# Layer 3's sums of neighbours as seven products of halves instead of eight

## Chip, cores and metric

The kernel runs on one core of one Trainium2 chip. The metric is the device time of one execution in microseconds, taken as the median of several runs. A profile of one execution goes with it.

## The reference

Four graph layers run one after the other over `x` (16 batches of 1024 nodes and 256 features) and `adj` (16 matrices of 1024 x 1024), all in float32. Each layer works on the normalised, rectified `x` and adds its result to `x`. The change lies in the last layer only:

```python
h = jnp.maximum(_layernorm(x, axis=-1), 0.0)
neighbor_sum = jnp.einsum('bnm,bmd->bnd', adjacency, h)
agg = epsilon * h + neighbor_sum
h = jnp.einsum('bnd,dh->bnh', agg, W1) + b1          # 256 -> 1024
h = jax.nn.silu(_rmsnorm(h, rms_weight))
out = jnp.einsum('bnh,hd->bnd', h, W2) + b2          # 1024 -> 256
x = x + out
```

## The kernel before

Layers 0 and 1 run first over all batches, then layer 2, which is a recurrence over the nodes, then layer 3 (`layer_3`, from L1093), which takes the last quarter of the time. Layer 3 is a loop over the 16 batches. For batch b it has these stages:

- **load** (L1130): the queue of SyncE fetches `x`, the layer-2 result `hn`, and the transposed adjacency in two halves of 512 columns, each a tile of 128 partitions x 8 row tiles x 512 (2 MB, four DMAs). The halves rotate over three buffers: two named `bxt`, one named `at`. A half is loaded when the products that read its buffer's last content are done.
- **prepare** (L1149): adds `hn` to `x` (VectorE, L1163), takes mean and variance (L1166, L1167), the inverse root on GpSimd (`rs`, L83), `shift` on VectorE (L1171), eight relus on ScalarE into `h` (L1173), and on GpSimd epsilon on the diagonal of the adjacency (L1154) and the output bias into `x` (L1177).
- **sums** (L1180): `agg` transposed, that is 256 features x 1024 nodes, as four parts (two halves of features by two halves of nodes). A part is eight products, one for each row tile, summed in a PSUM bank (L1189), copied to `ag` by ScalarE (L1191). VectorE forms the four differences `tt` that the next stage wants (L1195 to L1199).
- **inner** (L1202): the product with W1. It is written as seven products of halves in place of eight, in a loop of four steps with seven products each (L1210). `ws` and a changed quarter of W1 hold the combinations of the weights, made once (L1118 to L1121). Every result is evicted by VectorE into `hh` (L1214), with partial sums `u2` and `u3` (L1229, L1231) and ScalarE's copy `p1` (L1226). ScalarE squares each result (L1216, tile `sq`, two buffers) and GpSimd adds the squares up (L1218, 14 additions a batch). PSUM has five banks under the name `ph`, which sums and inner share.
- **norm** (L1241): four transposes for each of the two `ss` (L1250), a reduction (L1251), the inverse root on GpSimd, transposes of it (L1258), 16 scalings by VectorE (L1261) and 16 SiLUs by ScalarE (L1262).
- **outer** (L1265): the product with W2, again as seven products of halves with 16 small products each (L1279). VectorE makes the combinations of `hh` (L1273, eight operations of 128 x 1024, one of them into the buffer `s1`), and the results are added to `x` by VectorE and GpSimd (L1297 to L1312). The DMA of the output is issued from GpSimd's queue (L1337).

The loop of L1321 runs inner of batch b, then sums of batch b+1 with norm of batch b between its parts, then outer of batch b, which calls prepare of batch b+2 in its middle. The program is written in this order; the framework's scheduler then moves instructions on their engines by its own estimates of their durations, so the order of VectorE and GpSimd in the built program is not quite that of the text. [...]

Of the kernel before, what the change touches and what calls it, by code (L numbers as in the profile page):

```python
# [9 lines left out]
F32 = mybir.dt.float32  # L10
AF = mybir.ActivationFunctionType
ALU = mybir.AluOpType
# [4 lines left out]
P = 128  # L17
B, N, D, H = 16, 1024, 256, 1024
NT = N // P
DC = D // P  # L20
# [20 lines left out]
def gnn_stack(ctx: ExitStack, tc: tile.TileContext, a: dict, out: bass.AP):  # L41
    nc = tc.nc
# [29 lines left out]
    def rows(ap):  # L72
        return ap.rearrange("(t p) d -> p t d", p=P)
# [1019 lines left out]
    def layer_3(shared, x, hn, at, h, eye):  # L1093
        with ExitStack() as st:
            wp = st.enter_context(tc.tile_pool(name="w3", bufs=1))
            big = st.enter_context(tc.tile_pool(name="big3", bufs=2))
            small = st.enter_context(tc.tile_pool(name="small3", bufs=2))
            psum = st.enter_context(tc.tile_pool(name="psum3", bufs=2, space=PSUM))
# [14 lines left out]
            NH = 512  # L1113
# [3 lines left out]
            a11, a12, a21, a22 = (w1[:, c, p * HH * P : (p + 1) * HH * P] for p in range(2) for c in range(2))  # L1117
            nc.gpsimd.tensor_tensor(ws[:, 0], a21, a22, ALU.add)  # L1118
            nc.gpsimd.tensor_tensor(ws[:, 1], ws[:, 0], a11, ALU.subtract)
            nc.gpsimd.tensor_tensor(a21, a11, a21, ALU.subtract)  # L1120
            nc.gpsimd.tensor_tensor(ws[:, 2], a12, ws[:, 1], ALU.subtract)  # L1121

            wt = wp.tile([P, 3, HH, P], F32, name="wt")
# [6 lines left out]
            def load(b):  # L1130
                if b:
                    x[b] = big.tile([P, NT, D], F32, name="x", bufs=3)
                    nc.sync.dma_start(x[b], rows(x2_d[b]))
                    hn[b] = shared.tile([P, NT, D], F32, name="hb")
                    nc.sync.dma_start(hn[b][:, : NT - 1], rows(hn_d[b])[:, : NT - 1])
                    nc.sync.dma_start(hn[b][:, NT - 1], hs_d[NT - 1][b // GB][b % GB * P : (b % GB + 1) * P])
                    at[b] = []
                while len(at[b]) < N // NH:
                    n0 = NH * len(at[b])

                    if (2 * b + len(at[b])) % 3 < 2:
                        half = shared.tile([P, NT, NH], F32, name="bxt")
                    else:
                        half = big.tile([P, NT, NH], F32, name="at", bufs=1)
                    for t in range(0, NT, 2):
                        nc.sync.dma_start(half[:, t : t + 2], rows(a["adjT"][b])[:, t : t + 2, n0 : n0 + NH])
                    at[b].append(half)
# [29 lines left out]
                    nc.gpsimd.tensor_tensor(to[:, t : t + 2], x[b][:, t : t + 2], b2[:, None].to_broadcast([P, 2, D]), ALU.add)  # L1177
                x[b] = to

            def sums(b):  # L1180

                ag = big.tile([P, DC, N], F32, name="ag", bufs=1)
                tt = big.tile([P, 4, NH], F32, name="tt", bufs=1)
                b21 = []

                def part(n0, c):
                    pa = psum.tile([P, NH], F32, name="ph", bufs=5)
                    for mt in range(NT):
                        nc.tensor.matmul(pa, h[b][:, mt, c * P : (c + 1) * P], at[b][n0 // NH][:, mt],  # L1189
                                         start=mt == 0, stop=mt == NT - 1)  # L1190
                    nc.scalar.copy(ag[:, c, n0 : n0 + NH], pa)  # L1191
                    if (n0, c) == (0, 1):
                        b21.append(pa)
                    if (n0, c) == (NH, 0):
                        nc.vector.tensor_sub(tt[:, 0], pa, ag[:, 0, :NH])  # L1195
                    if (n0, c) == (NH, 1):
                        nc.vector.tensor_sub(tt[:, 1], pa, tt[:, 0])
                        nc.vector.tensor_sub(tt[:, 2], pa, ag[:, 0, NH:])
                        nc.vector.tensor_sub(tt[:, 3], b21[0], tt[:, 1])  # L1199
                return (ag, tt), [lambda n0=n0, c=c: part(n0, c) for n0 in range(0, N, NH) for c in range(DC)]  # L1200

            def inner(ag, tt):  # L1202

                hh = [big.tile([P, HC, NH], F32, name=f"hh{q}", bufs=1) for q in range(2)]
                ss = [small.tile([P, NH], F32, name=f"ss{q}", bufs=1) for q in range(2)]
                begun = [False, False]

                def product(lhsT, rhs, onto=None):
                    ph = onto if onto is not None else psum.tile([P, NH], F32, name="ph", bufs=5)
                    nc.tensor.matmul(ph, lhsT, rhs, start=onto is None, stop=True, skip_group_check=onto is not None)  # L1210
                    return ph

                def result(k, q, ph, u):
                    nc.vector.scalar_tensor_tensor(hh[q][:, k], ph, b1[:, k : k + 1], u, op0=ALU.add, op1=ALU.add)  # L1214
                    sq = small.tile([P, NH], F32, name="sq") if begun[q] else ss[q]
                    nc.scalar.activation(sq, hh[q][:, k], AF.Square)  # L1216
                    if begun[q]:
                        nc.gpsimd.tensor_tensor(ss[q], ss[q], sq, ALU.add)  # L1218
                    begun[q] = True

                left = lambda: None
                for k in range(HH):
                    mine = slice(k * P, (k + 1) * P)
                    p1, u2, u3 = (small.tile([P, NH], F32, name=name) for name in ("p1", "u2", "u3"))
                    ph = product(a11[:, mine], ag[:, 0, :NH])
                    nc.scalar.copy(p1, ph)  # L1226
                    left()
                    ph = product(ws[:, 1, mine], tt[:, 1])
                    nc.vector.tensor_add(u2, ph, p1)  # L1229
                    ph = product(a21[:, mine], tt[:, 2])  # L1230
                    nc.vector.tensor_add(u3, ph, u2)  # L1231
                    p5 = product(ws[:, 0, mine], tt[:, 0])
                    result(HH + k, 1, p5, u3)
                    result(HH + k, 0, product(a22[:, mine], tt[:, 3]), u3)
                    result(k, 0, product(a12[:, mine], ag[:, 1, :NH]), p1)
                    left = lambda k=k, mine=mine, p5=p5, u2=u2: result(
                        k, 1, product(ws[:, 2, mine], ag[:, 1, NH:], p5), u2)
                left()
                return hh, ss

            def norm(hh, ss):  # L1241

                got = {}

                def mean():
                    all_ = small.tile([P, N // P], F32, name="all")
                    for q in range(2):
                        pq = psum.tile([P, NH // P, P], F32, name="po", bufs=3)
                        for n in range(NH // P):
                            nc.tensor.transpose(pq[:, n], ss[q][:, n * P : (n + 1) * P], ident)  # L1250
                        nc.vector.tensor_reduce(all_[:, q * NH // P : (q + 1) * NH // P], pq, AX.X, ALU.add)  # L1251
                    got["rms"] = inv_sqrt(small, all_, RMS_EPS, [P, N // P], "rms", mul=1.0 / H)

                def spread():
                    for q in range(2):
                        pr = psum.tile([P, NH], F32, name="po", bufs=3)
                        for n in range(4):
                            nc.tensor.transpose(pr[:, n * P : (n + 1) * P],  # L1258
                                                got["rms"][:, 4 * q + n : 4 * q + n + 1].to_broadcast([P, P]), ident)
                        for k in range(HC):  # L1260
                            nc.vector.tensor_mul(hh[q][:, k], hh[q][:, k], pr)  # L1261
                            nc.scalar.activation(hh[q][:, k], hh[q][:, k], AF.Silu, scale=rw[:, k : k + 1])  # L1262
                return mean, spread
# [50 lines left out]
            load(0)  # L1314
            prepare(0)
            load(1)
            ags, parts = sums(0)
            for part in parts:
                part()
            prepare(1)  # L1320
            for b in range(B):  # L1321
                if b + 2 < B:
                    load(b + 2)
                hh, ss = inner(*ags)
                mean, spread = norm(hh, ss)
                parts = [lambda: None] * 4
                if b + 1 < B:
                    ags, parts = sums(b + 1)
                parts[0]()
                mean()  # L1330
                parts[1]()
                spread()
                parts[2]()
                parts[3]()

                outer(b, hh, (lambda: prepare(b + 2)) if b + 2 < B else (lambda: None))
                nc.gpsimd.dma_start(rows(out[b]), x[b])  # L1337

    layers_0_1()
    with tc.tile_pool(name="shared", bufs=2) as shared:  # L1340
        x, hn, at, h = {}, {}, {}, {}
# [49 lines left out]
```

## Time and profile before

| | |
|---|---|
| median of 3 runs | 4627.27 us (4623.85 to 4629.18) |
| span of the profiled execution, first to last instruction | 4622.5 us |
| median less that span | 4.8 us |
| TensorE busy, of the span | 4336.9 us (94%) |
| VectorE busy | 2535.5 us (55%) |
| GpSimd busy | 1623.5 us (35%) |
| ScalarE busy | 1279.5 us (28%) |
| first product of layer 3's sums | 3334.9 us |
| one batch of layer 3 in the steady state | 78.3 us |
| in it: TensorE, VectorE, GpSimd, ScalarE busy | 78.3, 51.6, 34.4, 28.9 us |
| granted clock of TensorE, mean | 0.978 |

The profiled execution's own time is its span with the launch and the end around it, which the records do not show; against the median of the runs these make up 4.8 us. A row of a timeline gives the start in us from the span's start, the duration in us, engine, line, operation, output and inputs with their shapes, how many in a row (x), and in brackets the idle time before it with what ended it. PE is TensorE, DVE VectorE, ACT ScalarE, POOL GpSimd. A float32 product stands in the records as two matmuls.

### The profile page before, as it was taken

How to read it: one execution, taken by the hardware profiler on the slowest of the kernel's cores; microseconds unless marked ns; L12 is line 12 of the kernel's file. 1: busy time of each engine (PE TensorE's matmuls, PEld its weight loads, DVE VectorE, ACT ScalarE, POOL GpSimd, SP SyncE). 2: the span in 40 equal slices, each digit the busy share in tenths (PEclk: the TensorE clock that was granted, in tenths of full speed). 3: DMA queues.
4: the chain of work that ended last, by engine and by line, in shares of the span. 5: the costliest groups of instructions: out<-in, count | busy, mean ns of one | idle time of the engine just before them, and what ended most of it. 6: DMA issues, size and time to landing. Idle time of an engine off the chain costs nothing. (4 is left out here: it accounts for less than half of the span.)

```text
span 4622.5 us, 54868 instructions
## 1 busy us (share of the span) xinstructions
PE 4336.9 (94%) x19223; PEld 2956.2 (64%) x19223; DVE 2535.5 (55%) x6436; ACT 1279.5 (28%) x2741; POOL 1623.5 (35%) x1914
## 2 busy tenths in 40 slices
PE   8999799999997899999999999999799999999998
PEld 4444345555554687778787878787655656565656
DVE  6667944555554344444444444445356666676765
ACT  1111111221121232323232323233234333333333
POOL 3222333433333333332332323234244444445352
PEclk9999899999998999999999999999899999999999
DMA  4333244455544644454444454542142222232310
GB/s 150 112 116 100 73 112 146 164 194 188 156 145 154 196 138 154 131 166 141 154 121 151 131 159 135 167 144 73 55 142 89 100 92 92 88 104 82 110 46 19
DMA packets 530989, 576.78 MB, mean 125 GB/s; under 512 B 42544, under 2 KB 439472, under 8 KB 528304
## 3 DMA queue, kind: packets, MB, share of 16 engines
q1 hardware_dynamic: 499536, 460.27, 32.0%
q0 software_dynamic: 31040, 111.44, 6.9%
q8 instruction: 206, 3.38, 0.3%
q14 instruction: 207, 1.70, 0.1%
HBM read 469.65 MB, written 116.65 MB: 127 GB/s over the span
## 5 line engine op out<-in xcount | busy, mean ns | idle before, releaser
L295 PE MATMUL pa<-at,h 128*128 128x512 f32 x1088 | 495.3, 608 | 33.0 <-DVE ag L300 33.0
L295 PE MATMUL pa<-at,q 128*128 128x512 f32 x960 | 423.6, 594 | 0.0
L623 PE MATMUL pf<-hb,ab 128*128 128x256 f32 x1568 | 407.9, 383 | 14.5 <-DMA hb<-hs_d 5.7
L295 PEld LDWEIGHTS pa<-at,h 128*128 128x128 f32 x1088 | 209.7, 196 | 277.6 <-issue 231.5
L735 PE MATMUL pf<-hs,wx 128*128 128x256 f32 x1536 | 348.9, 381 | 19.2 <-POOL hs L726 17.6
L735 PEld LDWEIGHTS pf<-hs,wx 128*128 128x128 f32 x1536 | 290.6, 191 | 62.5 <-POOL hs L726 19.4
L623 PEld LDWEIGHTS pf<-hb,ab 128*128 128x128 f32 x1568 | 280.3, 191 | 67.2 <-issue 14.2
L295 PEld LDWEIGHTS pa<-at,q 128*128 128x128 f32 x960 | 178.2, 190 | 215.9 <-issue 212.8
L1189 PE MATMUL ph<-bxt,hb 128*128 128x512 f32 x704 | 310.8, 597 | 3.8 <-ACT hb L1173 3.0
L1218 POOL TENSOR_TENSOR ss<-ss,sq 128x512 f32<-128x512 f32 x224 | 280.7, 1271 | 87.1 <-ACT sq L1216 83.4
L1023 POOL DMA_INDIRECT hs_d<-h,table x128 | 129.6, 1013 | 330.0 <-ACTq L1009 150.8
L1279 PEld LDWEIGHTS po<-w,hh 128*128 128x128 f32 x2048 | 235.9, 193 | 9.5 <-issue 7.2
L1279 PE MATMUL po<-w,hh 128*128 128x128 f32 x2048 | 240.1, 277 | 1.4 <-ACT hh L1262 0.7
L1189 PEld LDWEIGHTS ph<-bxt,hb 128*128 128x128 f32 x704 | 133.2, 192 | 164.7 <-issue 159.8
L740 DVE TENSOR_TENSOR gates<-pf,bias 128x512 f32<-128x512 f32 x128 | 88.3, 691 | 238.6 <-PE pf L735 238.6
L1261 DVE TENSOR_TENSOR hh<-hh,po 128x512 f32<-128x512 f32 x256 | 154.5, 681 | 96.7 <-PE po L1258 96.7
L83 POOL TENSOR_TENSOR rs<-rs_v,mhalf 128x8 f32<-128x8 f32 (+1 forms) x65 | 106.9, 1645 | 255.0 <-DVE rs_v L79 241.5
L771 PE MATMUL pf<-bd,h 128*128 128x384 f32 (+4 forms) x512 | 185.6, 454 | 5.3 <-ACT bs L610 2.8
L1216 ACT ACTIVATE sq<-hh 128x512 f32<-128x512 f32 x224 | 141.1, 630 | 164.3 <-DVE hh L1214 125.6
L830 ACT ACTIVATE r<-pr 128x256 f32<-128x256 f32 (+3 forms) x230 | 68.1, 348 | 403.5 <-PE pr L789 389.5
L1214 DVE SCALAR_TENSOR_TENSOR hh<-ph,b,u 128x512 f32<-128x512 f32 x192 | 144.0, 751 | 64.9 <-PE ph L1210 54.8
L774 DVE TENSOR_TENSOR bxt<-bxt,pf 128x384 f32<-128x384 f32 (+4 forms) x256 | 125.0, 501 | 97.0 <-PE pf L771 95.5
(296 smaller groups left out, 8473.1 us busy)
## 6 DMA issues: line engine op xcount, KB each, us to landing
at<-in_adjT SPq DMA_DIRECT2D x64, 1024.0 KB, 7.1
ab<-in_adj SPq DMA_DIRECT2D x128, 512.0 KB, 4.3
bxt<-in_adjT SPq DMA_DIRECT2D x88, 512.0 KB, 6.7
at<-in_adjT SPq DMA_DIRECT2D x40, 512.0 KB, 6.8
ad<-in_adj SPq DMA_DIRECT2D x128, 128.0 KB, 6.2
x_d<-x POOLq DMA_DIRECT2D x16, 1024.0 KB, 5.1
he_d<-h POOLq DMA_DIRECT2D x16, 1024.0 KB, 8.9
heT_d<-hT POOLq DMA_DIRECT2D x16, 1024.0 KB, 4.2
```

The source lines that it names most:

```text
L295: nc.tensor.matmul(pa, h[:, mt, c * P : (c + 1) * P], at[n0 // 512][:, mt], start=mt == 0, stop=mt == NT - 1)
L623: nc.tensor.matmul(pb, ab[:, jts[k]], hb[:, jts[k]], start=k == 0, stop=k == len(jts) - 1)
L735: nc.tensor.matmul(pg[:, e], wx[:, c, q * D + e * P : q * D + (e + 1) * P], self.hs[:, c], start=c == 0, stop=c == DC - 1)
L771: nc.tensor.matmul(pf, h[:, g, c * P : (c + 1) * P], bd[:, g, b0 : b0 + n, S : S + far], start=True, stop=True)
L774: return lambda: nc.vector.tensor_add(to, to, pf)
L1023: nc.gpsimd.indirect_dma_start(out=hs_d[t][g][:, :], out_offset=row(1, g, t, s), in_=h[:, g], in_offset=None)
L1189: nc.tensor.matmul(pa, h[b][:, mt, c * P : (c + 1) * P], at[b][n0 // NH][:, mt], start=mt == 0, stop=mt == NT - 1)
L1214: nc.vector.scalar_tensor_tensor(hh[q][:, k], ph, b1[:, k : k + 1], u, op0=ALU.add, op1=ALU.add)
L1216: nc.scalar.activation(sq, hh[q][:, k], AF.Square)
L1218: nc.gpsimd.tensor_tensor(ss[q], ss[q], sq, ALU.add)
L1261: nc.vector.tensor_mul(hh[q][:, k], hh[q][:, k], pr)
L1279: nc.tensor.matmul(po[:, n], left[:, c, n * P : (n + 1) * P], right[:, c], start=onto is None and n == 0 and c == 0, stop=c == HH - 1, ski ...
```

## The change

The sums of neighbours are written as seven products of quarters instead of eight. The 1024 source nodes and the 1024 target nodes of the adjacency are halved: b11, b21 are the upper and lower half of the rows of the left tile, b12, b22 those of the right tile. m0 and m1 are the two halves of the rows of `h`, each with two halves of columns. A product is now four matmuls of 128x128 by 128x512, and there are seven for a batch: 28 in place of 32.

- **Combinations of h** (`combined`): four subtractions or additions of 128 x 512 on GpSimd, three into the new tile `hs` and one in place.
- **Combinations of the adjacency**: b12 becomes b11 + b12 by a DMA from GpSimd's queue that adds to its destination within SBUF (L1199). t2 = that + b22, then t1 = t2 - b11 (in b12's place), then t2 = t2 + b21, all on VectorE in two operations of 128 x 1024 each (L1187). t2 lives in the buffer `s1` that outer uses too.
- **Results**: ScalarE makes three copies of 128 x 512 (before: four), VectorE seven evictions or subtractions (before: four). What is subtracted changes so that `tt` comes out negated in part, for which one combination of W1 changes its sign.
- **Order**: `combined` of batch b+1 is called ahead of inner of batch b; its two remaining steps, the DMA and t2, are handed to inner and called in the second and third step of its loop. In the built program the scheduler puts the DMA further ahead: on GpSimd behind `rms` of the batch before. It puts t2's two halves into VectorE's list behind `rs_v` and behind the second `u` of outer, and GpSimd's addition L1307 (now L1360) ahead of `rs`.

```diff
@@ -1117,7 +1117,7 @@
             a11, a12, a21, a22 = (w1[:, c, p * HH * P : (p + 1) * HH * P] for p in range(2) for c in range(2))
             nc.gpsimd.tensor_tensor(ws[:, 0], a21, a22, ALU.add)
             nc.gpsimd.tensor_tensor(ws[:, 1], ws[:, 0], a11, ALU.subtract)
-            nc.gpsimd.tensor_tensor(a21, a11, a21, ALU.subtract)
+            nc.gpsimd.tensor_tensor(a21, a21, a11, ALU.subtract)
             nc.gpsimd.tensor_tensor(ws[:, 2], a12, ws[:, 1], ALU.subtract)
 
             wt = wp.tile([P, 3, HH, P], F32, name="wt")
@@ -1177,29 +1177,80 @@
                     nc.gpsimd.tensor_tensor(to[:, t : t + 2], x[b][:, t : t + 2], b2[:, None].to_broadcast([P, 2, D]), ALU.add)
                 x[b] = to
 
-            def sums(b):
+            def quarters(b):
+                left, right = at[b]
+                return left[:, : NT // 2], right[:, : NT // 2], left[:, NT // 2 :], right[:, NT // 2 :]
+
+            def add(engine, to, left, right, op):
+                for k in range(0, NT // 2, 2):
+                    two = slice(k, k + 2)
+                    engine.tensor_tensor(to[:, two], left[:, two], right[:, two], op)
+
+            def combined(b):
+                b11, b12, _, b22 = quarters(b)
+                m0, m1 = h[b][:, : NT // 2], h[b][:, NT // 2 :]
+                hs = big.tile([P, 3, NT // 2, P], F32, name="hs", bufs=1)
+                nc.gpsimd.tensor_tensor(hs[:, 0], m0[:, :, P:], m1[:, :, P:], ALU.subtract)
+                nc.gpsimd.tensor_tensor(hs[:, 1], hs[:, 0], m0[:, :, :P], ALU.subtract)
+                nc.gpsimd.tensor_tensor(m0[:, :, P:], m0[:, :, :P], m0[:, :, P:], ALU.subtract)
+                nc.gpsimd.tensor_tensor(hs[:, 2], m1[:, :, :P], hs[:, 1], ALU.add)
+                t2 = big.tile([P, NT // 2, NH], F32, name="s1", bufs=1)
+                return (t2, hs), [lambda: nc.gpsimd.dma_start(b12, b11, accum_op=ALU.add),
+                                  lambda: add(nc.vector, t2, b12, b22, ALU.add)]
+
+            def sums(b, t2, hs):
 
                 ag = big.tile([P, DC, N], F32, name="ag", bufs=1)
                 tt = big.tile([P, 4, NH], F32, name="tt", bufs=1)
-                b21 = []
-
-                def part(n0, c):
-                    pa = psum.tile([P, NH], F32, name="ph", bufs=5)
-                    for mt in range(NT):
-                        nc.tensor.matmul(pa, h[b][:, mt, c * P : (c + 1) * P], at[b][n0 // NH][:, mt],
-                                         start=mt == 0, stop=mt == NT - 1)
-                    nc.scalar.copy(ag[:, c, n0 : n0 + NH], pa)
-                    if (n0, c) == (0, 1):
-                        b21.append(pa)
-                    if (n0, c) == (NH, 0):
-                        nc.vector.tensor_sub(tt[:, 0], pa, ag[:, 0, :NH])
-                    if (n0, c) == (NH, 1):
-                        nc.vector.tensor_sub(tt[:, 1], pa, tt[:, 0])
-                        nc.vector.tensor_sub(tt[:, 2], pa, ag[:, 0, NH:])
-                        nc.vector.tensor_sub(tt[:, 3], b21[0], tt[:, 1])
-                return (ag, tt), [lambda n0=n0, c=c: part(n0, c) for n0 in range(0, N, NH) for c in range(DC)]
-
-            def inner(ag, tt):
+                b11, t1, b21, b22 = quarters(b)
+                m0, m1 = h[b][:, : NT // 2], h[b][:, NT // 2 :]
+                got = {}
+
+                def product(left, right, onto=None):
+                    pa = onto if onto is not None else psum.tile([P, NH], F32, name="ph", bufs=5)
+                    for k in range(NT // 2):
+                        nc.tensor.matmul(pa, left[:, k], right[:, k], start=onto is None and k == 0, stop=k == NT // 2 - 1,
+                                         skip_group_check=True)
+                    return pa
+
+                def room(name):
+                    return small.tile([P, NH], F32, name=name)
+
+                def first():
+                    got["pa"] = product(m0[:, :, :P], b11)
+                    got["p1"] = room("p1")
+                    nc.scalar.copy(got["p1"], got["pa"])
+                    got["p5"] = product(hs[:, 0], t1)
+                    add(nc.vector, t1, t2, b11, ALU.subtract)
+
+                def second():
+                    p6 = product(hs[:, 1], t2)
+                    got["u2"] = room("u2")
+                    nc.vector.tensor_add(got["u2"], p6, got["p1"])
+                    add(nc.vector, t2, t2, b21, ALU.add)
+                    product(m1[:, :, :P], b21, got["pa"])
+                    nc.scalar.copy(ag[:, 0, :NH], got["pa"])
+
+                def third():
+                    p7 = product(m0[:, :, P:], t1)
+                    got["u3"] = room("u3")
+                    nc.vector.tensor_add(got["u3"], p7, got["u2"])
+                    nc.vector.tensor_sub(ag[:, 1, NH:], got["p5"], got["u3"])
+                    pa = product(m1[:, :, P:], t2)
+                    nc.vector.tensor_add(ag[:, 1, :NH], pa, got["u3"])
+                    got["p7"] = p7
+
+                def fourth():
+                    p7 = got["p7"]
+                    product(hs[:, 2], b22, p7)
+                    nc.scalar.copy(tt[:, 2], p7)
+                    nc.vector.tensor_sub(tt[:, 1], ag[:, 0, :NH], p7)
+                    nc.vector.tensor_sub(tt[:, 0], ag[:, 1, NH:], tt[:, 1])
+                    nc.vector.tensor_sub(tt[:, 3], ag[:, 1, :NH], tt[:, 1])
+                return (ag, tt), [first, second, third, fourth]
+
+            def inner(ag, tt, between):
 
                 hh = [big.tile([P, HC, NH], F32, name=f"hh{q}", bufs=1) for q in range(2)]
                 ss = [small.tile([P, NH], F32, name=f"ss{q}", bufs=1) for q in range(2)]
@@ -1235,6 +1286,8 @@
                     result(k, 0, product(a12[:, mine], ag[:, 1, :NH]), p1)
                     left = lambda k=k, mine=mine, p5=p5, u2=u2: result(
                         k, 1, product(ws[:, 2, mine], ag[:, 1, NH:], p5), u2)
+                    if k and between:
+                        between.pop(0)()
                 left()
                 return hh, ss
 
@@ -1314,18 +1367,22 @@
             load(0)
             prepare(0)
             load(1)
-            ags, parts = sums(0)
-            for part in parts:
+            of, adds = combined(0)
+            ags, parts = sums(0, *of)
+            for part in adds + parts:
                 part()
             prepare(1)
             for b in range(B):
                 if b + 2 < B:
                     load(b + 2)
-                hh, ss = inner(*ags)
+                adds = []
+                if b + 1 < B:
+                    of, adds = combined(b + 1)
+                hh, ss = inner(*ags, adds)
                 mean, spread = norm(hh, ss)
                 parts = [lambda: None] * 4
                 if b + 1 < B:
-                    ags, parts = sums(b + 1)
+                    ags, parts = sums(b + 1, *of)
                 parts[0]()
                 mean()
                 parts[1]()
```

## Prediction

> **What bounds the kernel now.** The change touches layer 3 alone, so I read that layer from the end backwards: first the chain of work that ended last, cut to one batch in the middle.
>
> ```profile
> 3963.86 13.74 PE ph L1189 x32
> 3977.59 25.06 PE po L1279 x224
> 4002.65 24.04 PE ph L1210 x56
> 4026.69 6.87 PE ph L1189 x16
> ```
>
> TensorE goes from piece to piece without a gap, and every batch repeats this after 78.3 us (3400.2, 3478.5, 3556.8). A float32 product stands in the records as two matmuls; 32 records last 13.74 us, so a 128x128 by 128x512 product costs 0.859 us. A batch is 32 products of sums (27.5), two groups of transposes (1.7), outer (25.1) and inner (24.0). VectorE is busy 51.6 us of the 78.3, GpSimd 34.4, ScalarE 28.9: TensorE is the bound, and four products fewer are worth 3.43 us a batch if nobody else becomes late.
>
> Second, who else is tight. Call Z the start of inner's first product, 4002.49 in this batch. The timeline of GpSimd around it:
>
> ```profile
> 3995.65 1.65 POOL L83 TENSOR_TENSOR rs<-rs_v,mhalf 128x8 f32<-128x8 f32 x1 [8.13 <-DVE rs_v L79]
> 3997.28 1.26 POOL L1307 TENSOR_TENSOR x<-x,u 128x512 f32<-128x512 f32 x1
> 3999.77 3.73 POOL L1177 TENSOR_TENSOR x<-x,b 128x512 f32<-128x512 f32 x3 [1.23 <-ACT hb L1173]
> 4003.46 1.27 POOL L1309 TENSOR_TENSOR x<-x,u 128x512 f32<-128x512 f32 x1
> 4004.68 1.27 POOL L1310 TENSOR_TENSOR x<-x,u 128x512 f32<-128x512 f32 x1
> 4005.91 1.27 POOL L1177 TENSOR_TENSOR x<-x,b 128x512 f32<-128x512 f32 x1
> 4007.12 0.93 POOL L1337 DMA_DIRECT2D out<-x  x1
> 4009.41 1.26 POOL L1218 TENSOR_TENSOR ss<-ss,sq 128x512 f32<-128x512 f32 x1 [1.35 <-ACT sq L1216]
> ```
>
> GpSimd works here almost without a break, and is free for the sums of squares (L1218) only at Z+5.6; the first starts at Z+6.9. There are 14 of them at 1.27 us, four in each 6.0 us of inner. ScalarE, in the same batch:
>
> ```profile
> 4015.05 0.63 ACT L1216 ACTIVATE sq<-hh 128x512 f32<-128x512 f32 x1 [0.59 <-POOL ss L1218]
> 4015.59 0.57 ACT L1226 COPY p<-ph 128x512 f32<-128x512 f32 x1
> ```
>
> A square waits for GpSimd's sum, because sq has two buffers; behind it in ScalarE's order stands the eviction of inner's next product (L1226), and TensorE has five ph buffers. So a late GpSimd stops TensorE. Today the slack just holds.
>
> Third, VectorE's step that releases the next batch's relu:
>
> ```profile
> 3995.40 0.17 DVE L79 TENSOR_SCALAR rs_v<-mv 128x8 f32<-128x8 f32 x1
> 3995.54 0.69 DVE L1288 TENSOR_TENSOR u<-po,p 128x512 f32<-128x512 f32 x1
> 3997.34 1.23 DVE L1171 SCALAR_TENSOR_TENSOR shift<-mv,rs 128x8 f32<-128x8 f32 x1 [1.10 <-POOL rs L83]
> ```
>
> shift has eight elements and takes 1.23 us; over all batches it is 0.16 at the least and 1.23 in the median. It ends at 3998.57, when GpSimd's L1307 (3997.28 + 1.26) ends.
>
> [...]a combine of L1273 at 3985.27 took 1.53 instead of 1.22 beside L1154. [...]the trace's 1 MB out<-x lands after 5.2. [...]No run here shows an accumulating DMA yet.
>
> **Part by part.** *Removed:* four products in each of 16 sums, 3.43 us each; with transposes, outer and inner unchanged the period could be 74.9. In sums, one ScalarE copy of 0.59 us goes. The sign of a21 costs nothing.
>
> *VectorE, added per batch:* six adds of 128x1024 at 1.21 (as L1273) and three more evictions or subtractions at 0.60 (the pace of L1261): about 9 us, 60 of 74.9; room on average. The t1 add goes ahead of the mean's reduction (two at 1.2, after the sums' eighth product): rms is then ready about 12.6 us after sums begin, the transposes that need it stand at 14.6. Nothing lost; 2 us of cover remain. The b21 add ends at 14.4, just ahead of the scalings of hh (L1261). After those scalings (which start 0.64 after the second transposes and last 9.66) VectorE has eight 512-wide operations (4.8) and eight combines (9.5), one behind the other, before x21 is done. From the second transposes to Z lie 0.87 + 6.87 + 3.43 + 25.06 = 36.2 us, so x21 ends at Z-11.6, and Z-10.7 with some 0.9 of L1154[...]; before: Z-13.4. Thus VectorE's tail is 2.7 us later against TensorE, with no TensorE wait yet.
>
> *The wait that follows.* The changed program's order of instructions differs around Z. GpSimd has x12+=u2 ahead of rs. VectorE has u2, rs_v, the first half of t2, shift, u3, the second half of t2. Prepare's 6.4 us and u2 end at Z-3.8. Then[...]: x12 to Z-2.5, half of t2 (1.21) to Z-1.3, rs (1.65) to Z+0.35, shift to Z+0.5. ScalarE's eight relus (4.04) end at Z+4.55, before Z+0.15. VectorE: u3, then t2's second half to Z+2.35. GpSimd behind it: x21 and x22 to 4.85, three L1177 to 8.55, the output DMA to 9.6, the last L1177 to 10.85. New there: four combinations of h, which wait for relu and stand ahead of the sums of squares. I price them as L1118's 1.26, at a pace of 1.24: 5.0 us, to Z+15.8. Behind them queue all squares' sums: the first starts at 15.8 instead of 6.9.
>
> *What that costs.* The eviction L1226 of the third step of inner's loop stands behind the fifth buffered square, which needs the third sum: 15.8 + 3.8 = 19.6, square and eviction 1.2, so Z+20.8. TensorE's 20th product of inner needs that buffer at 19 x 0.859 = Z+16.3. It waits 4.5, and about 0.4 more accrue where a product is added onto one whose eviction is late. Inner becomes 28.9 instead of 24.0. In general inner grows by T - 10.9, where T is when the first sum of squares starts. Net 4.9 - 3.43 = +1.5 us a batch. The last of 14 sums is done at about Z+33.6; transposes ask at 28.9 + 6.9 = 35.8: no further wait.
>
> *The accumulating DMA:* it is issued after the right half's first pieces have landed, about 7 us after the second transposes (as L1154's 3969.98 against 3962.82), so Z-29 or so, while GpSimd idles; issue 0.93 as L1337. t2 asks for it at Z-2.5: cover 25 us. [...]I take 10, cost nothing. No row bounds it above; beyond 25 us every microsecond is paid in each batch. A gain is excluded, since nothing else speeds up. The s1 buffer, now shared with t2, makes outer's first combine wait for sums' sixth product, which ends 3 us before VectorE is through with the scalings and gets there: nothing.
>
> *Counted out.* Inners of batches 1 to 14 have this pattern: 14 x 1.5 = +20. Batch 15 has no combinations, and batch 0's sums wait for other things: hs0 after relu (3347.4), and batch 1's hn, whose buffer L1177 frees at 3357.2 and now four combinations (5 us) later; that puts inner(0) off by about 1, and its own stall, against 1.7 us of idle there now, takes about 4 more; sums(1) gives 3.4 back: +2. Together +22. The profiled span is 4622.5, 4.8 below the median of 4627.3 (launch and end lie outside it; that part stays). Forecast 4627 + 22 = 4649.
>
> **Rivals.** *A, faster:* the place is the few microseconds around Z[...], so T is earlier. [...]x12 and rs run through to Z-1.7, relu ends at 2.5, and T is about 12.5: inner grows 1.6, net -1.8, 14 x -1.8 = -25, 4604. It decides from T < 14.3. For it: TensorE's own saving is certain; against it: shift's 1.23. *B, late DMA:* it takes 30 us or more and t2, shift and relu wait: +5 a batch more, about 4719. For it: adding inside SBUF is unseen here; against it: 25 us of cover. *C, full gain:* GpSimd's combinations fall into gaps: 15 x 3.43, 4578. Against it: they stand ahead of the first sum, with no gap left. *D, even:* T of 13.7 to 14.9, 4618 to 4636.
>
> **Chances.** A change of 0.2% (9 us) is about what measuring this kernel can tell from none. Forecast (T from 15 to 17.5, 4637 to 4675) 0.55; D 0.15; A 0.14; C 0.03; B 0.13. Faster 0.17, same 0.15, slower 0.68. The range 4605 to 4690 leaves out C, half of A at most, the slow part of B. The slower cases' own range is 4637 to 4690.
>
> **What would show it.** Lines are those of the changed program. Right: a period near 79.8 us; 28 products (24.05 us) in sums; inner of 28 to 30 us with its wait on ScalarE's copy L1277 at the 20th product; ScalarE waiting for GpSimd's L1269; first L1269 near Z+15.8; shift at or after Z. Wrong: L1269 near Z+12 and a period below 78 (A); VectorE's L1187 waiting for the DMA (B); GpSimd's combinations well off 1.24 us each, every 0.1 us being 0.4 a batch, 6 in all.

## The result, and the profile after

The changed kernel takes 4674.96 us, the median of 4 runs (4668.2 to 4687.48), against 4626.27 of the kernel before in the same comparison: a ratio of 1.0107, 95% interval 1.0086 to 1.0128. Run again later beside the last experiments it gave 4679.94 against 4624.21, 1.0114 (1.0098 to 1.0131). It is slower by about 50 us, where 22 were forecast: the direction and the place were right, the forecast size was less than half of the measured one.

The profiled execution has a span of 4666.5 us, 44.0 more than before. The layers ahead of layer 3 reach it 8.6 us earlier in this profile (first L1118 at 3332.15 instead of 3340.71). Over the profiles of this study, the same code ahead of layer 3 ended anywhere from 3332 to 3349, and at 3344.87 in the second profile of the same kernel, so that is chance. Layer 3 itself is 52.6 us longer, and I count only there. From sums to sums a batch takes 81.35 us in the mean instead of 78.31, which makes 14 x 3.04 = +42.5; the start and the end make up +10.1.

First the chain of work that ended last, from the end of one batch's outer into the next inner (start, duration, what; Z, the start of inner's first product, is 3943.89 here):

```profile
3939.95 0.17 DVE rs_v L79
3940.11 2.24 POOL x L1360
3942.36 1.62 POOL rs L83
...
3944.86 2.18 POOL x L1362
...
3948.24 3.73 POOL x L1177 x3
3951.96 0.93 POOL out L1394
...
3954.21 1.23 POOL hs L1194
...
3959.24 2.45 POOL ss L1269 x2
...
3963.58 0.58 ACT p L1277
...
3964.20 10.55 PE ph L1261 x20
```

Before, TensorE followed TensorE on this chain. Now it leaves TensorE ahead of Z and runs for 23 us through GpSimd's queue: x12, rs, x21, b2's additions, the output DMA, the combinations of h, three sums of squares. Only then come ScalarE's eviction and TensorE. ScalarE in the same batch, from its timeline:

```profile
3944.22 4.04 ACT L1173 ACTIVATE hb<-x,shift,rs 128x256 f32<-128x256 f32 x8 [20.53 <-DVE shift L1171]
...
3960.49 0.63 ACT L1267 ACTIVATE sq<-hh 128x512 f32<-128x512 f32 x1 [6.40 <-POOL ss L1269]
3961.71 0.63 ACT L1267 ACTIVATE sq<-hh 128x512 f32<-128x512 f32 x1 [0.59 <-POOL ss L1269]
3963.05 0.63 ACT L1267 ACTIVATE sq<-hh 128x512 f32<-128x512 f32 x1 [0.71 <-POOL ss L1269]
3963.58 0.57 ACT L1277 COPY p<-ph 128x512 f32<-128x512 f32 x1
```

The wait of a square for GpSimd, 0.59 us before, has become 6.40, and the copy of the third step stands behind three squares that wait. TensorE, same batch:

```profile
3955.55 1.88 PE L1261 MATMUL ph<-ag,w 128*128 128x512 f32 x4
...
3959.84 1.02 PE L1261 MATMUL ph<-tt,ws 128*128 128x512 f32 x2
3964.20 1.43 PE L1261 MATMUL ph<-tt,w 128*128 128x512 f32 x2 [3.34 <-ACT p L1277]
3965.43 3.31 PE L1261 MATMUL ph<-ag,w 128*128 128x512 f32 x4
```

There are two things to see. The 19th product (3964.20) waits 3.34 us for ScalarE's copy, the wait that was forecast for the 20th. And the four records behind it take 3.31 us, where four took 1.88 before the wait. The stretches of the same batch say why (columns: stretch, its length, busy time of TensorE and records, the granted clock, then the load of the DMA engines and their GB/s, which don't matter here):

```profile
3956.00:3960.70 4.70, 4.70 (x12) 1.00 0.55 161
3964.20:3968.60 4.40, 4.40 (x7) 0.61 0.01 2
3968.60:3974.60 6.00, 6.00 (x16) 1.00 0.00 0
```

After the wait TensorE ran 4.4 us at a granted clock of 0.61, then at 1.00 again. That term was in no sum of mine.

### The profile page after: what moved, and what is told of

Its sections match the earlier page's. It is cut to its first block, busy times and chain, and to the rows that moved or that the text cites. A ratio compares the mean times of both kernels' runs of the same rounds, so it can differ in the third digit from the quotient of the medians.

```text
span 4666.5 us, 55029 instructions
## 1 busy us (share of the span) xinstructions
PE 4308.3 (92%) x19095; PEld 2929.3 (63%) x19095; DVE 2658.5 (57%) x6580; ACT 1268.4 (27%) x2725; POOL 1797.2 (39%) x1994
## 5 line engine op out<-in xcount | busy, mean ns | idle before, releaser
L1332 PEld LDWEIGHTS po<-w,hh 128*128 128x128 f32 x2048 | 236.6, 193 | 16.6 <-issue 14.1
L1261 PE MATMUL ph<-tt,w 128*128 128x512 f32 x256 | 139.1, 626 | 50.4 <-ACT p L1277 49.3
L300 DVE COPY ag<-pa 128x512 f32<-128x512 f32 x64 | 44.0, 687 | 243.1 <-PE pa L295 242.9
L847 DVE TENSOR_TENSOR w<-w,hc 128x256 f32<-128x256 f32 (+3 forms) x230 | 87.4, 380 | 139.0 <-ACT hc L846 139.0
L1265 DVE SCALAR_TENSOR_TENSOR hh<-ph,b,u 128x512 f32<-128x512 f32 x192 | 139.7, 748 | 45.9 <-PE ph L1261 37.6
```

Of the source, the lines that this page charges most:

```text
L1332: nc.tensor.matmul(po[:, n], left[:, c, n * P : (n + 1) * P], right[:, c], start=onto is None and n == 0 and c == 0, stop=c == HH - 1, ski ...
```

## The experiments

Eleven runs were made. My theory: the start of the sums of squares, T after Z, decides; it is late because GpSimd has more queued ahead of it, and takes longer beside VectorE's t2 additions (x12 takes 2.25 us, in the kernel before 1.26); TensorE's wait and the low clock follow from that. Rivals: the accumulating DMA, the extra work of VectorE by itself, and a slow stretch with a cause other than idleness. The unmodified changed kernel ran a second time:

> The changed kernel itself, once more beside the others. Period 81.3, 4668 to 4682; the start of layer 3 in the profile, 3332 in the first one, shows how much the layers ahead of it vary from run to run (3332 to 3349 over the kernels so far, in which they are the same).

It came to 4679.94, a period of 81.32, and 3344.87 for the start of layer 3.

**The four combinations of h left out.** The three hs tiles are replaced by views of h.

```diff
-                hs = big.tile([P, 3, NT // 2, P], F32, name="hs", bufs=1)
-                nc.gpsimd.tensor_tensor(hs[:, 0], m0[:, :, P:], m1[:, :, P:], ALU.subtract)
...
+                hs = (m0[:, :, P:], m1[:, :, P:], m1[:, :, :P])
```

> The changed kernel without the four combinations of h on GpSimd; the halves of h itself go into the products (this leaves out part of the computation). Theory: T is 5.0 us earlier, Z+10.3 instead of 15.3; nothing waits at the 19th product and the clock holds: period 75 to 76.3, 4578 to 4597. Rival 1 (accumulating DMA, VectorE's adds): 4660 to 4680, since both stay. Rival 2 (relu is late[...]): relu is as late as before, and about half of the growth of inner stays, 4620 to 4640.

Measured: 4594.54, ratio to before 0.9927 (0.9905 to 0.9948), period 75.94, inner 25.2 with no wait at the 19th product. Some 80 us come back, 76 of them in the steady batches (14 x 5.41), for 14 x 5 us of GpSimd's time, with the DMA and all of VectorE's additions still in place.

**The accumulating DMA left out.**

```diff
-                return (t2, hs), [lambda: nc.gpsimd.dma_start(b12, b11, accum_op=ALU.add),
+                return (t2, hs), [lambda: None,
```

> The changed kernel without the accumulating DMA: b12 goes into the products as it was loaded (this leaves out the first combination of adj's halves). Theory (GpSimd's late queue is the whole cost; the DMA lands under 25 us of cover and nobody waits for it): period 81.3 to 81.5 in layer 3 as in the changed kernel, half-speed stretch included, 4660 to 4680. Rival (its megabyte of traffic inside SBUF, or its issue on GpSimd, slows loads, products or GpSimd): period down by 1 us or more, 4655 or less.

Measured: 4676.79, 1.0111 (1.0088 to 1.0135), period 81.30 against 81.35 and 81.32: in the steady batches it costs nothing. In the changed kernel its issue took 0.92 us on GpSimd while GpSimd waited anyway. In the batch shown above it was issued at 3913.78 and its reader t2 started at 3940.01 without a wait. It had landed long before: all its packets, the only ones of GpSimd's queue there (1.05 MB), lie between 3915.25 and 3921.65, so it was done 7.9 us after its issue; the 10 us of the prediction were an estimate, which no run had shown. Only at the start is it not covered: for batch 1 it was issued at 3371.04, and t2 waited 2.19 us for it, until 3381.66. Without the DMA, inner of batch 0 took 43.0 us in the profile instead of 45.0 and 45.9.

**The kernel before, with GpSimd made late and nothing else.**

```diff
+            def combined(b):
+
+                m0, m1 = h[b][:, : NT // 2], h[b][:, NT // 2 :]
+                hs = big.tile([P, 3, NT // 2, P], F32, name="hs", bufs=1)
+                for k in range(7):
+                    nc.gpsimd.tensor_tensor(hs[:, k % 3], m0[:, :, P:], m1[:, :, :P], ALU.add)
...
+                if b + 1 < B:
+                    combined(b + 1)
                 hh, ss = inner(*ags)
```

> The kernel before with seven additions of 128x512 on GpSimd that nobody reads, where the changed kernel has its combinations of h; no other part of the change. 7 x 1.24 = 8.7 us, so that T moves from Z+6.9 to about 14.3 to 15.6. Theory (T alone decides): the eviction that TensorE waits for ends at T + 5.0, the 19th product wants it at Z + 15.5: a wait of 3.8 to 5.1, 0.5 more behind it, and 1.4 of half clock[...]: inner 24.0 becomes 29.7 to 31, period 84 to 85.3, 4626 + 14 x 5.7 to 7 = 4706 to 4724. Without a clock term: 4687 to 4705. Rival (VectorE's later tail or the DMA is needed for the stall): period under 80, under 4650.

Measured: 4704.97, 1.0175 (1.0156 to 1.0193), period 83.75; just under the span that I gave with the clock term, and right at the top of that without it. Z is 3962.91; GpSimd and TensorE in one batch:

```profile
3967.43 7.43 POOL L1185 TENSOR_TENSOR hs<-hb 128x512 f32<-128x512 f32 x6
...
3976.98 7.62 POOL L1225 TENSOR_TENSOR ss<-ss,sq 128x512 f32<-128x512 f32 x6
```

```profile
3982.00 2.08 PE L1217 MATMUL ph<-tt,w 128*128 128x512 f32 x2 [3.47 <-ACT p L1233]
3983.87 2.43 PE L1217 MATMUL ph<-ag,w 128*128 128x512 f32 x4
```

T is 14.1, and the same product waits for the same copy. So the stall needs neither the DMA nor VectorE's additions. The clock fell as well, in all 14 batches: in this one it stood at 0.50 from the product's start at 3982.00 to 3984.96, then at 1.00. Inner came to 29.2 to 29.6 in 13 batches and 30.85 in one, in which the clock stayed low for twice as long.

**TensorE kept at work in its wait.**

```diff
+                    if k == 2:
+                        po = psum.tile([P, NH], F32, name="po", bufs=3)
+                        for _ in range(3):
+                            nc.tensor.matmul(po, a22[:, mine], tt[:, 0], start=True, stop=True)
                     result(HH + k, 0, product(a22[:, mine], tt[:, 3]), u3)
```

> The changed kernel with three additional products, whose result nobody reads, on TensorE ahead of inner's 19th product, where it waits for 3.4 us: 2.57 us of work into a wait. Theory of the clock (the half-speed stretch after the wait comes from TensorE having stood idle): the idle time falls to 0.8 us, the clock stays at 1.00 after it, the products behind it run at 0.43 a record; period 81.4 becomes 79.7, 4648, although TensorE does 36 us more work. Rival (the products after the wait are slow because of what the other engines do there[...]): no gain, 4670 to 4675; if the added products don't fall into a wait, they cost 2.57 a batch, 4705.

Measured: 4657.79, 1.0064 (1.0043 to 1.0086), period 80.09. The kernel does more on TensorE and is some 20 us faster than the changed one (4657.79 against 4674.96 and 4679.94). The interval of its ratio to before and that of the changed kernel's first measurement touch at 1.0086, so the profile has to say it:

```profile
3958.52 2.74 PE L1288 MATMUL po<-tt,w 128*128 128x512 f32 x6
3962.03 1.13 PE L1261 MATMUL ph<-tt,w 128*128 128x512 f32 x2 [0.77 <-ACT p L1277]
3962.99 1.88 PE L1261 MATMUL ph<-ag,w 128*128 128x512 f32 x4
```

The product starts at Z+20.3 as in the changed kernel, since ScalarE's copy is no earlier, but the four records behind it take 1.88 instead of 3.31. Inner is 29.3 to 29.7 in 13 of 14 batches and 28.5 in the last, instead of 30.7 as a rule: in this kernel the slow stretch comes from the idle time, and it costs 1.4 us. In the changed kernel itself two of the 14 batches kept the clock after the same 3.35 us of idle time, and had inners of 29.3 as well.

**A third buffer for the squares.**

```diff
-                    sq = small.tile([P, NH], F32, name="sq") if begun[q] else ss[q]
+                    sq = small.tile([P, NH], F32, name="sq", bufs=3) if begun[q] else ss[q]
```

> The changed kernel with three buffers for the squares instead of two. Theory (GpSimd's late start on the sums of squares, T, stops ScalarE, and ScalarE's late eviction stops TensorE at inner's 19th product): ScalarE may run one square further ahead, so the eviction L1277 that TensorE waits for stands behind the second sum of squares instead of the third, 1.27 us earlier. The wait of 3.4 us becomes 2.2; if such a shorter wait leaves the clock at full speed, the 1.8 us after it go as well. Inner 30.7 becomes 27.7 (29.4 if the clock still drops), the period 81.4 becomes 78.4 (80.1): 4630 (4655). Rival 1 (the accumulating DMA or VectorE's adds slow the period down by themselves): the number of squares changes nothing, 4665 to 4680.

Measured: 4640.07, 1.0029 (1.0018 to 1.0041), period 78.74. The copy stands behind one addition less, so the product starts at Z+19.0 instead of 20.3 after 2.0 us of wait, and the clock held in 12 of 14 batches: inner 27.65 as a rule, 29.65 in one whose clock fell.

**The t2 additions away from Z.**

```diff
-                    if k and between:
+                    if k == 1 and between:
                         between.pop(0)()
+                    if k == 2 and between:
+                        with tc.issue_after(last[0].ins):
+                            between.pop(0)()
```

Here `last[0]` is the addition that makes u3 in the same step of inner.

> The changed kernel with VectorE's two additions for t2 (L1187) queued behind the third step's u3 in inner, instead of being taken up around Z[...]. Theory[...]: x12 takes 1.3 instead of 2.25, rs comes 1.2 earlier, relu ends at Z+3.2 instead of 4.4; the early waits of 1.4 us in inner fall to 0.6 or less; x21 takes 1.3; T comes at Z+12.7 to 13.5 instead of 15.3. Two additions of 1.2 then stand against sums of squares inside inner and give up to half of it back. The wait at the 19th product falls to 1.5 to 2.5[...]: period 77.5 to 79.3, 4610 to 4645. Rival 1 (the four combinations alone are the cost[...]): T stays over 14.5, period over 80, 4655 or more. Rival 2 (the additions in inner cost as much as those around Z): period 81, 4668.

Measured: 4663.85, 1.0087 (1.0069 to 1.0104), period 80.54. Around Z all went as expected: x12, with no addition of t2 beside it, took 1.27 us instead of 2.25, relu ended at Z+3.4, T came at 13.3, the early waits went, and the wait at the 19th product was 2.3. The expected period has a full clock behind such a wait, which was my estimate: in eight of the 14 batches the clock still fell (the four records behind the product took 2.56 to 3.52 us), and in six, such as this one, it stayed at 1.00 (1.88 us). In these the two additions gave back what was won (VectorE, then TensorE):

```profile
3970.68 2.30 DVE L1187 TENSOR_TENSOR s<-at 128x1024 f32<-128x1024 f32 x1
3972.91 1.40 DVE L1265 SCALAR_TENSOR_TENSOR hh<-ph,b,u 128x512 f32<-128x512 f32 x2
...
3974.88 1.98 DVE L1187 TENSOR_TENSOR s<-at 128x1024 f32<-128x1024 f32 x1
```

```profile
3973.70 1.13 PE L1261 MATMUL ph<-ag,ws 128*128 128x512 f32 x2 [1.56 <-DVE hh L1265]
```

Beside GpSimd's sums of squares they took 2.30 and 1.98 instead of 1.21, the evictions of hh came late, and TensorE waited 1.56 and 0.71 for them. Where the clock had fallen, the slower products hid the first of these two waits, and inner took 29.8 us as a rule in either case. An addition moved off one path lay on another: rival 2 was right on the total.

**b2's additions moved behind the last sum of squares,** where GpSimd idles. They are first needed by outer.

```diff
-                to = x[b] if b else big.tile([P, NT, D], F32, name="x", bufs=3)
...
+                if b == 0:
+                    bias(b)
...
                 hh, ss = inner(*ags, adds)
+                if b + 1 < B:
+                    with tc.issue_after(sums_of_squares[-1].ins):
+                        bias(b + 1)
```

`bias` holds the four lines taken out of `prepare`.

> The changed kernel with GpSimd's four additions of b2 (L1177) queued behind the last sum of squares of inner, when GpSimd idles, instead of ahead of the combinations of h. Theory: combinations start when relu ends, Z+4.4, and T comes at Z+9.4 to 10.4 instead of 15.3, below the 10.9 from which inner grows. No wait at the 19th product, no low clock after it; of the 6.7 us by which inner grew at most the early 1.4 stay. Period 74.9 to 76.3: 4575 to 4597. Rival 1 (DMA traffic, VectorE): the waits stay, 4660 to 4680. Rival 2 (what is late is relu[...], and GpSimd's queue only follows): inner keeps about half of its growth, 4620 to 4640.

Measured: 4605.96, 0.9959 (0.9945 to 0.9973): faster than both kernels. GpSimd, with Z at 3923.82:

```profile
3928.63 0.98 POOL L1403 DMA_DIRECT2D out<-x  x1 [0.30 <-POOL x L1369]
3929.64 1.29 POOL L1198 TENSOR_TENSOR hs<-hb 128x512 f32<-128x512 f32 x1
...
3934.70 2.51 POOL L1275 TENSOR_TENSOR ss<-ss,sq 128x512 f32<-128x512 f32 x2
```

T is 10.9 (10.8 in most batches), later than the 9.4 to 10.4 that I gave, since the output DMA stands ahead of the combinations. Still nothing waits at the 19th product (but in the first of the batches, 1.3 us). The time is above my 4575 to 4597, because I subtracted from the one profiled run of the changed kernel, which lay some 7 us below its median; the period, 76.26, is at the top of what I gave. Inner is 25.4: the early waits of 1.36 us stay, at the 6th and 8th product, behind ScalarE's first copy, which stands behind relu.

**Three moves at once, in a version that I took for the best.** b2's additions behind the last square, t2 inside inner (both as above), and on VectorE:

```diff
-            prepare(1)
+            with tc.issue_after(last_of_sums[0].ins):
+                prepare(1)
```

> The changed kernel with three moves in the order of work: b2's additions behind the last sum of squares (as in the run with the bias moved), the t2 additions inside inner (as in the run with t2 late), and prepare of batch 1 on VectorE behind the last subtraction of sums of batch 0, so that inner of batch 0 does not wait 11 us for it. Theory: T comes at Z+8 to 9.5, relu ends at Z+3.2, the early waits of 1.4 fall to 0.6 or less and the period to 74.9 to 75.5; at the start up to 8 us less. 4622 + 14 x (75.2 - 78.3) - 3.4 = about 4580 (4570 to 4595), faster than both kernels and than the bias alone (4606). Rival (the additions of t2 inside inner meet the sums of squares, and stop ScalarE there): period 76.5 or more, 4600 to 4615.

Measured: 4616.82, 0.9987 (0.9980 to 0.9995), period 76.88: slower than b2's additions moved alone. The rival was right on the batches, for the reason seen with t2 late. The third move missed as well: the first subtractions of inner of batch 0 wait only 0.54 us, but the order on GpSimd changed as well. There the additions to the diagonal of batch 1's second half (L1154), which wait 9.68 us for a load, now stand ahead of the combinations of h and not behind them; the first square's sum starts at 3401.57, 33 us after that inner began, TensorE waits 11.52 us for ScalarE's copy, and inner of batch 0 takes 47.3 us instead of 45.0. It ran beside the run with t2 late, before that was known.

**b2 moved and relu freed.** b2's additions moved as in the run above, and two edges of order more: GpSimd's x12 behind rs, VectorE's t2 behind shift. `power[0]` is the instruction of rs, `last_shift[0]` that of shift.

```diff
+                with tc.issue_after(power[0].ins):
+                    nc.gpsimd.tensor_tensor(x12, x12, u2, ALU.add)
...
+                        with tc.issue_after(last_shift[0].ins):
+                            between.pop(0)()
```

> The changed kernel with b2's additions behind the last sum of squares, as in the run with the bias moved (4606), and two more edges of order: on GpSimd x12 += u2 behind rs, on VectorE the two additions for t2 behind shift. [...]Theory: rs starts at once behind rs_v (about Z-4.4) and ends near Z-2.8, shift follows, relu ends at Z+1.6 to 2 instead of 4.4; the early waits of 1.36 us, all that is left of inner's growth in that run, go: inner 24.0 to 24.3, period 74.9 to 75.2, another 14 x 1.1 to 1.4 = 15 to 19 us: 4585 to 4592. Rival (the early waits come from ScalarE's or GpSimd's own order, not from a late relu): period 76.2, 4604 to 4608.

Measured: 4593.35, 0.9932 (0.9916 to 0.9949), period 75.35, inner 24.46, each a little above what I gave. rs starts at once, but x12 now runs beside shift, which takes 1.23 us instead of the 0.17 of the changed kernel and ends when x12 does, at 3916.46 and 3916.44 (Z is 3917.25; GpSimd, then VectorE):

```profile
3913.53 1.66 POOL L83 TENSOR_TENSOR rs<-rs_v,mhalf 128x8 f32<-128x8 f32 x1 [7.18 <-DVE rs_v L79]
3915.18 1.26 POOL L1372 TENSOR_TENSOR x<-x,u 128x512 f32<-128x512 f32 x1
```

```profile
3915.23 1.23 DVE L1175 SCALAR_TENSOR_TENSOR shift<-mv,rs 128x8 f32<-128x8 f32 x1 [1.77 <-POOL rs L83]
```

So relu ends at Z+3.3, not at the 1.6 to 2 that I gave, and 0.4 us of the early delay are left.

**The start in another order.** The combinations of W2 come behind b2's additions for batch 0.

```diff
                     bias(b)
+                    with tc.issue_after(biased[0].ins):
+                        weights()
```

`weights` holds the four lines L1125 to L1128.

> The same with the order at the start changed too: the four combinations of W2 (L1125 to L1128) behind b2's additions for batch 0, whose end frees the buffer that batch 1's hn is loaded into; VectorE waits for that load ahead of the subtractions that inner of batch 0 needs (10.9 us of TensorE's idle time in the changed kernel, 4.8 in the kernel before). Theory: hn starts up to 8 us earlier and so does all that follows: 4577 to 4587. Rival (inner of batch 0 is held by GpSimd's sums of squares anyway): no change against the run without it.

Measured: 4588.43, 0.9919 (0.9902 to 0.9935), just above 4577 to 4587. Inner of batch 0 takes 38.1 us instead of 42.8, with 6.12 us of idle time instead of 10.86 for the same subtraction. The medians are 4.9 us apart, with intervals that overlap, so that the gain rests on the 4.7 us of one profile each. This version is 36 us faster than the kernel before and 91 faster than the changed one (4588.43 against 4679.94, measured side by side).

## Why the prediction was right or wrong

**What held.** TensorE's saving is there: the period without inner is 50.8 us (81.5 - 30.7), 3.5 less than before (54.3). VectorE's tail came as computed: x21 ended at 3933.28, Z-10.6 (10.7 forecast). One choice differed: the first t2 half was taken before x12 rather than behind it. The length was the same, x12 paying for it with 2.25 us instead of 1.26 (that the two would take turns was my estimate from shift's 1.23 us), and shift ended at Z+0.3 (0.5), relu at Z+4.4 (4.55). On GpSimd x21 took 2.18, the four combinations 5.0 (5.0), and T was 15.3 (15.8). ScalarE's copy ended at Z+20.3 (20.8). The accumulating DMA cost nothing in the steady batches (rival B falls); the 10 us taken for it were enough. Rival A, in which x12 and rs run through, falls: x12 took 2.25 us beside t2's first half, and 1.27 with t2 late.

**The step that failed** is "What that costs", with its "Inner becomes 28.9 instead of 24.0". Inner became 30.7 as a rule. Its terms, against what was measured:

| term of inner | forecast | measured |
|---|---|---|
| T, from which the copy follows 5.0 us later | 15.8 | 15.3 (-0.5) |
| the product that waits for the copy | the 20th | the 19th, so 0.86 us of work more lies behind the wait |
| clock after the wait | full (0) | 0.61 for 4.4 us: +1.4 |

28.9 - 0.5 + 0.86 + 1.4 = 30.7. The measured start of the 19th product was T + 5.0 in each of three kernels: 15.3 and 20.3, 14.1 and 19.1 (the kernel before made late), 13.3 and 18.3 (t2 late). The remaining ten products take 24.04 - 18 x 0.859 = 8.6 us, and 0.4 accrue: 20.3 + 8.6 + 0.4 = 29.3, which is what inner took whenever the clock held. That the 19th product waits, not the 20th, holds for the kernel before as well, as the run of it with GpSimd made late shows; why the built program gives it that bank, no run shows. The early waits at the 6th and 8th product, which I had not listed, cost nothing as long as this later wait swallows them; they cost 1.36 us once it is gone.

The clock is what I should have asked about. In the profiles of the kernel before and of the changed one the granted clock is 1.00 or 0.50, and it changes only at steps of 3.41 us. In that of the changed kernel, from the second batch of layer 3 on, it fell from 1.00 to 0.50 at 13 of these steps, and each time TensorE had been at work for 1.21 us or less of the step just past. At 339 it stayed at 1.00, and there TensorE had been at work for 1.56 us or more. In the kernel before it fell once, after 1.35 us of work, and stayed at 351 steps, after 2.74 or more. So what counted in these batches is how a wait lay against the steps. The changed kernel shows both cases after a wait of 3.3 us (columns as above): the batch shown, with the step that the wait leaves almost empty and the step after it, and a batch that kept the clock, because the wait fell in two steps:

```profile
3961.48:3964.89 3.41, 0.69 (x2) 1.00 0.16 53
3964.89:3968.31 3.42, 3.42 (x6) 0.50 0.01 2
4121.91:4125.33 3.42, 1.94 (x5) 1.00 0.85 281
4125.33:4128.74 3.41, 1.56 (x4) 1.00 0.01 2
```

How often the clock fell behind the 19th product, by the length of the wait there: 0.77 us in none of 14 batches (TensorE kept at work), 2.0 in two (three buffers for the squares), 2.3 in eight (t2 late), 3.3 in 11 (DMA left out), about 3.35 in 12 (each profile of the changed kernel), 3.5 in all 14 (the kernel before made late). In the layers ahead, with other products, it also fell after up to 1.91 us of work in a step (2.16 in the kernel before). I had forecast an idle time of 4.5 us, longer than any of these waits.

The two terms are worth 2.3 us a batch, less 0.5 for T: 14 x 1.8 = 25 us; 22.5 were measured (42.5 against 20), since two batches kept the clock.

**The start** was mis-sized too. "+2" was forecast for the start and batch 0, after its 3.4 of saving; measured +10.1. From the first L1118 to the start of inner of batch 0 it is 28.1 us (28.2 before), so "puts inner(0) off by about 1" was not so. But TensorE waits 10.93 us there for VectorE's first subtraction, instead of 4.78: VectorE's addition ahead of it waits for batch 1's hn, whose buffer b2's additions free 27.3 us after the first L1118 instead of 16.5. Of that 10.8, 5 are the combinations of h, as I had it, and most of the rest is GpSimd's longer work beside VectorE's t1 and t2 additions at the start: three combinations of W2 took 2.25 us each instead of 1.26. The last experiment's 4.7 us show this path. Inner of batch 0 grew by 13.9 us in all (45.0 against 31.1); most of the rest is five later waits, 5.7 us together, where about 4 were forecast.

**Together:** forecast +20 for the batches and +2 for the start; measured in layer 3 +42.5 and +10.1.

## What to carry to other kernels

Before a stage gets new work on an engine that is "mostly idle", look for what stands behind it in that engine's queue: four GpSimd additions, 5 us in a batch where GpSimd is busy 46 of 81, cost some 80 us because the sums of squares stood behind them, and the work that nobody needed yet (b2) was the thing to move. When you price a wait of TensorE, price the clock after it as well (1.4 us a batch here), and take which product waits from a run that makes it wait, if there is one: the count of banks was one product off. An instruction moved off a path can cost as much where it lands: beside the sums of squares t2's two additions took 2.30 and 1.98 us instead of 1.21. Look who is beside it there.

## What the runs showed of the hardware that was not expected

An SBUF-to-SBUF accumulating DMA of 1 MB costs its issuer 0.92 us, and leaving it out moved the period by 0.05 us or less. In the batch shown its packets ran from 1.5 to 7.9 us after the issue, those of the plain 1 MB out<-x from 1.6 to 4.8: about half the rate.

With 2.6 us of work whose result nobody reads in its wait of 3.4, TensorE kept its pace behind the wait in all 14 batches (1.88 us for four records, at a clock of 1.00 in the batch shown), which saved 1.4 us a batch. And the length of a wait alone did not decide the drop: 3.35 us kept the clock in two batches of 14, while 2.0 us lost it in two and 2.3 in eight. In the batches of the changed kernel's profile it fell when TensorE had worked for 1.21 us or less of one 3.41-us step, and stayed after 1.56 or more.
